# A graph-attention kernel on one core: gathers into the tile of three superchunks before, chunk by chunk behind the sums, instead of into a new tile

## Chip, core and metric

The kernel runs on one core of a Trainium2 chip. The metric is the device time of one execution in microseconds (us). Engines are named as in the profile: PE (TensorE, matmul), DVE (VectorE), ACT (ScalarE), POOL (GpSimd), SP (SyncE, DMA issue).

## The reference

Two graph-attention (GAT) layers over one graph of 6250 nodes with 256 features and 200 000 edges, which come sorted by destination `dst`, with 32 features on each edge. Layer 0 has 4 heads, layer 1 one.

```python
h = relu(layernorm(x))
for each layer:
    te = relu(edge_attr @ We + be) * exp(x @ Wo + bo)[src]      # 64 wide
    # self loops are added, each with the mean of its node's te
    hx, he = x @ Wg, te @ Wge
    al = leaky_relu((hx·a_s)[src] + (hx·a_d)[dst] + he·a_e, 0.2)
    al = exp(al - segment_max(al, dst)[dst]);  al /= segment_sum(al, dst)[dst]
    x  = segment_sum(hx[src] * al, dst) + b + x                 # relu behind layer 0
return input + h_after_both
```

So each edge needs the transformed row `hx[src]` of its source, weighted by a softmax over the edges of its destination, and summed per destination.

## The kernel before

The node rows of a layer stand in a table `T` in device memory (`T0`, `T1` for the layers): 256 features and a few columns that the logits need, 268 numbers a row in layer 0 and 260 in layer 1. The edges are cut into 1563 chunks of 128, and these into superchunks of C = 24, 66 in a layer (the last two of a layer have 17 and 10 chunks). A superchunk is a step; the 132 steps of both layers are numbered k = 0 to 131, and layer 1 begins with step 66.

What a step does:

- `gather` (L1066, POOL): one indirect DMA for each chunk, which brings 128 rows of `T`, picked by the edges' `src`, into `G[:, c, :]`. `G` is 128 x 24 x 270 float32. Three pools with one buffer each (`gath0` to `gath2`, `self.gp`) hold these tiles; step k uses pool k % 3, so steps k and k+3 share their memory. POOL's stream of instructions is little else than gathers.
- `logits`, `ends`, `links`, `maxima` (DVE, with short transposes on PE, L1305, L1371, L1388, L1564 among them): logits and the running maximum of each destination, by scans over sorted edges (L1381 is one of the scans).
- `scale` (layer 0, DVE, L1455) or `scale_rows` (layer 1, ACT, L1464): the gathered rows are multiplied by their weights.
- `onehots` (DVE, L1284): a one-hot matrix `S` of 128 x 128 for each chunk, from edge to node of the superchunk's window.
- `sums` (PE, L1474): 24 matmuls, one for each chunk, `u += S[c].T @ G[c]`, 48 records in the trace. They are the last readers of `G`.
- `evict` (ACT, L1479): `u` from PSUM to `U` in SBUF. The profile's chains end in this wait most often.
- `finish` of the step before, and `edge_rows` (PE, ACT: L1166, L1167, L1175) for the next: work that fills in between.

The loop over the steps is `edges`. In iteration k it calls `gather` for step k+1. POOL has its own queue and no other work, so a gather starts as soon as its waits allow; the program's order on the other engines doesn't hold it. Every DMA of POOL also waits for one of eight completion semaphores (DMASW0 to 7, used in turn).

A step's tile of `G` is made in one of two ways. Ordinarily it is a new tile of its pool. The first gather into it then waits for the whole tile of the step three before to be free: for PE's last sum of that step, and for DVE. This first gather is that of the last chunk; the rest follow in order 0 to 22. For steps 3, 4 and 5, and for some at the seam of the layers (steps 66, 68 and 69, in `ending` and `sources`), `st["own"]` names the older tile itself, and `gather` goes through the chunks in order 0 to 23. Each gather is then an ordinary overwrite of one chunk, and waits for that chunk's last reader alone.

A sum that something waits for increments PE's semaphore. In layer 0 most superchunks of before have one increment of 24 behind the last sum; behind the sums of layer 1, and of layer 0's steps 0 to 2, it is one of 1 behind each.

Of the kernel before, what the change touches and what calls it, by code (L numbers as in the profile page):

```python
# [81 lines left out]
class Kernel:  # L82
# [705 lines left out]
    def edges(self, ctx):  # L788
        nc = self.nc
        steps = self.steps  # L790
        if self.NS % 2:
            self.load_lb(1)
        pv = late = None
        self.ahead, self.rest = 1, None
        for k, st in enumerate(steps):
            nx = steps[k + 1] if k + 1 < len(steps) else None
            if st["s"] + 2 >= self.NS:
                continue
            for q in steps[k + 1:k + 3]:
                if q["L"] is st["L"] and "tw" not in q:  # L800
                    self.nodes(q)
            self.load_lb(k + 2)
            left = 99
            if self.ahead < len(self.groups):
                left = self.groups[self.ahead][0] - 2 - (self.ahead + 2 >= len(self.groups)) - k
            if self.rest is None and left <= 2:
                gi = self.index_load(self.ahead, self.xp)
                self.rest = self.index_group(self.ahead, self.xp, gi)
            if st["L"].l and (st["s"] == 2 or st["s"] + 3 == self.NS) and not hasattr(self, "flag_i"):
                self.flag()  # L810
                if self.early:
                    self.window()
            if st["s"] + 3 == self.NS:
                self.ending(st, *steps[k + 1:k + 3], pv, late, steps[k + 3] if k + 3 < len(steps) else None)
                pv = late = None
                continue
            if 3 <= k + 1 < 6 and nx["L"].l == 0:
                nx["own"] = steps[k - 2]["G"]
            if k:
                self.gather(nx)  # L820
                st["rows"] = st["L"].l
                drain(self.logits(st))
                self.ends(st)
            self.spread(nx)
            self.parts(nx)
            y = self.rphase1(nx)
            next(y)
            if k:
                self.links(st)
            if late:  # L830
                self.rows2(late)
            self.load_fl(k + 1)
            self.blocks(nx)
            if k:
                drain(self.maxima(st))
            drain(y)
            self.load_ea(k + 2)
            self.rphase2(nx)
            self.adst(nx)
            if "S" not in st:  # L840
                self.onehots(st)
            if k:
                if st["rows"]:
                    self.scale_rows(st)
                else:
                    drain(self.scale(st))
                self.carried(st)
                self.sums(st)
            if late:
                self.rows3(late)  # L850
                late = None
            self.onehots(nx)
            if pv:
                drain(self.finish(pv))
            self.evict(st)
            if pv:
                self.rows1(pv)
                late = pv
            self.index_on(left)
            if k == 4 and self.early:  # L860
                self.lacking()
            if k >= 6:
                next(self.late, None)
                next(self.late, None)
            self.edge_rows(nx)
            if st["s"] + 4 == self.NS:
                drain(self.finish(st))
            pv = st
# [186 lines left out]

    def gather(self, st):
        nc, L = self.nc, st["L"]
        own, G = "own" in st, st.get("own")
        if not own:
            G = self.G0 if st["k"] == 0 else self.gp[st["k"] % 3].tile([P, C, 270], F32, name="G")  # L1060
        st["G"] = G
        idx = self.src[:, st["o"]:st["o"] + st["C"]]
        last = st["C"] - 1
        c0 = (self.CX, self.CX1, 0)[min(st["k"], 2)]
        for c in range(last + 1) if own else (last, *range(c0, last)) if c0 <= last else ():
            nc.gpsimd.indirect_dma_start(  # L1066
                out=G[:, c, 0:L.TW], out_offset=None, in_=st.get("from", self.T[L.l])[0:self.N, :],
                in_offset=bass.IndirectOffsetOnAxis(ap=idx[:, c:c + 1], axis=0))
# [688 lines left out]
def drain(g):  # L1757
    for _ in g:
        pass
# [85 lines left out]
```

## Time and profile before

| | |
|---|---|
| time, median of 3 runs | 4930.62 us (4925.73 to 4934.31) |
| profiled execution | 4919.58 us |
| its span, first to last instruction | 4917.8 us |
| mean granted TensorE clock | 0.729 |
| busy: PE / PE weight load / DVE / ACT / POOL | 2927.7 / 1837.1 / 2461.0 / 1132.4 / 2988.8 us |
| gathers on POOL (L1066) | 3066 + 24, mean 950 ns |

The profile is of one execution; its page has been read together with answers of the trace: waits (the group that waited and its releaser, then us in total, times, longest us), groups of instructions by line, and timelines of an engine within a window. In a timeline a row begins with the start and the duration in us, and the bracket holds the idle time of the engine ahead of it and what ended it. "issue" is time in which the engine waited for nothing that the profile shows; "remote" is a releaser that it could not name.

### The profile page before, as it was taken

The page shows a single profiled execution, that of the slowest core. Times are in us where ns is not written, and L with a number is a line of the kernel's source. Part 1 is how long each engine was busy: PE and PEld are TensorE (multiplying, and loading weights), DVE is VectorE, ACT ScalarE, POOL GpSimd, SP SyncE. Part 2 cuts the span into 40 slices and gives each one's busy share as a digit, 9 for nine tenths or more (in the row PEclk, how much of TensorE's full clock was granted, in tenths as well). Part 3 has the DMA queues.
Part 4 walks back from the last instruction along what each step waited for, and adds up shares of the span by engine and source line. Part 5 has one row for each costly group of instructions (what it writes and reads, how often), then busy time and mean ns, then how long its engine had stood idle before and what let it go on. Part 6 is the DMA issues. An engine that isn't in the chain of part 4 may idle for free.

```text
span 4917.8 us, 38116 instructions
## 1 busy us (share of the span) xinstructions
PE 2927.7 (60%) x10100; PEld 1837.1 (37%) x10100; DVE 2461.0 (50%) x6148; ACT 1132.4 (23%) x2703; POOL 2988.8 (61%) x3216
## 2 busy tenths in 40 slices
PE   6656666666665666565646556555565555555556
PEld 5433433334343434343434333333333333333334
DVE  5556666666766666666744333333333332333335
ACT  4211111111111111111103333233332333323332
POOL 5356666666666666666554656666666665666663
PEclk8777777777777777777777666667676666766667
DMA  7144444444444444444433434444444443444442
GB/s 223 55 121 121 128 130 135 124 132 134 131 126 128 136 125 132 128 135 123 122 110 93 122 106 116 120 114 111 112 119 114 113 123 105 116 120 111 115 115 71
DMA packets 248252, 591.96 MB, mean 120 GB/s; under 512 B 65849, under 2 KB 105125, under 8 KB 247783
## 3 DMA queue, kind: packets, MB, share of 16 engines
q0 software_dynamic: 150048, 422.51, 32.8%
q1 hardware_dynamic: 97009, 164.82, 10.6%
q10 hardware_dynamic: 976, 2.12, 0.2%
q8 instruction: 86, 1.41, 0.1%
q14 instruction: 133, 1.09, 0.1%
HBM read 544.23 MB, written 45.36 MB: 120 GB/s over the span
## 4 chain that ended last, share of the span: by engine, by line
PE 30%; issue 28%; DVE 22%; POOL 10%; another core or an unknown queue 6%; DMA 2%; ACT 2%; DVEq 0%; ACTq 0%; POOLq 0%
PE u L1474 22%; POOL G L1066 10%; DVE G L1455 8%; PE y L1166 3%; DMA G<-T,src 2%; DVE S L1284 2%; PE zad L1175 2%; DVE m L1403 1%; PE ps L567 1%; DVE lb L1190 1%; ACT R L1167 1%; DVE rt L1333 1%; DVE fb L1398 0%; PE zad L1319 0%
## 5 line engine op out<-in xcount | busy, mean ns | idle before, releaser
L1066 POOL DMA_INDIRECT G<-T,src x3066 | 2913.0, 950 | 1817.8 <-issue 950.7
L1474 PE MATMUL u<-G,S 128*128 128x270 f32 (+1 forms) x6232 | 1866.5, 446 | 1421.0 <-issue 1194.1
L1474 PEld LDWEIGHTS u<-G,S 128*128 128x128 f32 x6232 | 1355.1, 220 | 1857.8 <-issue 1392.1
L1464 ACT ACTIVATE G<-G,kw 128x256 f32<-128x256 f32 x1512 | 609.0, 496 | 0.0
L1381 DVE TENSOR_TENSOR_SCAN cl<-fl,cl,lf 4x129 f32<-4x129 f32 (+1 forms) x130 | 61.1, 470 | 999.3 <-PE zad L1305 928.9
L1479 ACT ACTIVATE U<-u 128x270 f32<-128x270 f32 (+1 forms) x131 | 51.4, 393 | 2164.8 <-PE u L1474 1622.8
L1455 DVE TENSOR_TENSOR G<-G,kps 128x6144 f32<-128x6144 f32 (+6 forms) x86 | 441.7, 5149 | 0.0
L1284 DVE TENSOR_TENSOR S<-kps,loc 128x3072 f32<-128x3072 f32 (+1 forms) x135 | 438.1, 3245 | 4.7
L1166 PE MATMUL y<-ea,webd 64*128 64x256 f32 (+2 forms) x1056 | 355.2, 763 | 41.8 <-ACT R L1167 33.9
L1175 PE MATMUL zad<-R,wea 128*64 128x384 f32 (+1 forms) x1056 | 279.5, 666 | 156.6 <-ACT R L1167 84.9
L1167 ACT ACTIVATE R<-y,webd 128x1024 f32<-128x1024 f32 (+3 forms) x264 | 235.4, 892 | 428.3 <-PE y L1166 159.8
L1175 PEld LDWEIGHTS zad<-R,wea 128*64 128x64 f32 x1056 | 81.8, 174 | 392.5 <-issue 234.5
L1506 DVE SCALAR_TENSOR_TENSOR mg<-U,mw 128x1 f32<-128x1 f32 x66 | 14.6, 221 | 369.2 <-remote 160.7
L1166 PEld LDWEIGHTS y<-ea,webd 64*128 64x128 f32 x1056 | 115.9, 269 | 106.2 <-issue 60.3
L1333 DVE STREAM_TRANSPOSE rt<-zad 128x768 f32<-128x768 f32 (+1 forms) x130 | 125.8, 967 | 5.0 <-remote 5.0
L567 PE MATMUL fin<-wg,h1T 128*128 128x260 f32 x264 | 116.5, 586 | 1.6 <-ACT h1T L1566 1.6
L1190 DVE TENSOR_TENSOR lb<-lb,kps 128x1536 bf16<-128x1536 bf16 (+1 forms) x68 | 112.9, 1661 | 0.0
L1437 DVE SCALAR_TENSOR_TENSOR G<-U,kw,G 1x257 f32<-1x257 f32 x62 | 29.5, 476 | 152.5 <-issue 78.5
L1576 ACT ACTIVATE t1rows<-t1rows 128x1 f32<-128x1 f32 x66 | 13.4, 203 | 365.2 <-DVE crow L1443 144.3
L1564 PE MATMUL fin<-ident,fb 128*128 128x128 f32 x132 | 42.7, 379 | 79.9 <-issue 78.3
L1371 PE MATMUL lf<-ident,fb 128*36 128x128 f32 (+1 forms) x132 | 52.0, 394 | 59.9 <-DVE fb L1364 56.9
L1516 ACT ACTIVATE mw<-mw 128x8 f32<-128x8 f32 x66 | 13.8, 209 | 299.9 <-issue 137.9
(264 smaller groups left out, 2402.9 us busy)
## 6 DMA issues: line engine op xcount, KB each, us to landing
ea<-in_ea_dram SPq DMA_DIRECT2D x64, 768.0 KB
G<-T,src POOLq DMA_INDIRECT x3066
lb<-locrow SPq DMA_DIRECT2D x64, 384.0 KB
nd<-t1rows SPq DMA_DIRECT2D x66, 225.8 KB
tw<-nd SPq DMA_DIRECT2D x66, 225.8 KB
tw<-T SPq DMA_DIRECT2D x66, 117.2 KB
T<-t1rows SPq DMA_DIRECT2D x66, 113.8 KB
tw<-in_x_dram SPq DMA_DIRECT2D x66, 112.0 KB
```

What stands on the lines that cost most here:

```text
L567: self.nc.tensor.matmul(ps[:, :L.MW], hT[:, k, :], self.wg[L.l][:, k, :], start=(k == 0), stop=(k == 1))
L1066: nc.gpsimd.indirect_dma_start(out=G[:, c, 0:L.TW], out_offset=None, in_=st.get("from", self.T[L.l])[0:self.N, :], in_offset=bass.Indirect ...
L1166: nc.tensor.matmul(y[:, i, :n], self.webd[l][r, :], ea[r, w], start=True, stop=True)
L1167: nc.scalar.activation(R[:, :, w], y[:, :, :n], AF.Relu, bias=self.be[l])
L1175: nc.tensor.matmul(st["zad"][i * PH:(i + 1) * PH, o], self.wea[l][0], R[:, i, w], start=True, stop=False)
L1190: V.tensor_tensor(lb[:, :, :n], lb[:, :, :n], self.k_part.unsqueeze(2).to_broadcast([P, i, n]), op=OP.is_equal)
L1284: nc.vector.tensor_tensor(st["S"][:, c0:c1, :], self.k_iota.unsqueeze(1).to_broadcast(w), self.loc[:, o + c0:o + c1].unsqueeze(2).to_broad ...
L1333: V.transpose(rv[:, :32 * c].rearrange("p (b n) -> p b n", b=2), z.rearrange("p (b n) -> p b n", b=2)[:, :, :16 * c])
L1381: V.tensor_tensor_scan(cl[:H, :], fl[:H, :], lf[:H, 0:P + 1], init, op0=OP.add, op1=OP.max)
L1455: nc.vector.tensor_tensor(v, v, pw[:, c0:c1, :].unsqueeze(3) .to_broadcast([P, c1 - c0, H, L.F]), op=OP.mult)
L1464: self.nc.scalar.activation(v, v, AF.Copy, scale=st["w"][:, c:c + 1])
L1474: nc.tensor.matmul(st["u"][:, :L.W], S[:, i, :], G[:, i, 0:L.W], start=(j == 0), stop=(j == c - 1))
```

## The change

`gather` itself now sets `own` for every step above 2 that doesn't have it yet, to the tile of the step three before, and the place in `edges` that set it for steps 3 to 5 goes. So from the fourth superchunk on, in both layers, no new tile of `G` is taken, the chunks come in order 0 to 23, and each gather waits for PE's sum of the same chunk, three superchunks before.

```diff
@@ -814,8 +814,6 @@
                 self.ending(st, *steps[k + 1:k + 3], pv, late, steps[k + 3] if k + 3 < len(steps) else None)
                 pv = late = None
                 continue
-            if 3 <= k + 1 < 6 and nx["L"].l == 0:
-                nx["own"] = steps[k - 2]["G"]
             if k:
                 self.gather(nx)
                 st["rows"] = st["L"].l
@@ -1055,6 +1053,8 @@
 
     def gather(self, st):
         nc, L = self.nc, st["L"]
+        if st["k"] > 2 and "own" not in st:
+            st["own"] = self.steps[st["k"] - 3]["G"]
         own, G = "own" in st, st.get("own")
```

The order of instructions on PE, DVE, ACT and SP is the same in both programs. On POOL the same gathers are issued, with the last chunk of each superchunk at its end and no longer at its start, and with other waits. POOL, before, from one superchunk of layer 0 into the next (`G_2899`, `G_3076` are the two tiles, `T0_60` the table of layer 0, the list behind "waits" the semaphores):

```order
L1066 DMA G_2899<-T0_60,src_177 128x268 [waits DMASW7_49]
L1066 DMA G_3076<-T0_60,src_177 128x268 [waits DMASW0_49,DVE_49,PE_49]
L1066 DMA G_3076<-T0_60,src_177 128x268 [waits DMASW1_49]
L1066 DMA G_3076<-T0_60,src_177 128x268 [waits DMASW2_49]
L1066 DMA G_3076<-T0_60,src_177 128x268 [waits DMASW3_49]
L1066 DMA G_3076<-T0_60,src_177 128x268 [waits DMASW4_49]
```

The second row is the gather of the last chunk, and the only one that waits for PE. At the same place in the program after the change (`G_1912` and `G_206` are tiles of earlier superchunks, used again):

```order
L1066 DMA G_1912<-T0_60,src_177 128x268 [waits DMASW7_49,PE_49]
L1066 DMA G_206<-T0_60,src_177 128x268 [waits DMASW0_49,PE_49]
L1066 DMA G_206<-T0_60,src_177 128x268 [waits DMASW1_49,PE_49]
L1066 DMA G_206<-T0_60,src_177 128x268 [waits DMASW2_49,PE_49]
L1066 DMA G_206<-T0_60,src_177 128x268 [waits DMASW3_49,PE_49]
L1066 DMA G_206<-T0_60,src_177 128x268 [waits DMASW4_49,PE_49]
```

Every gather now has a wait on PE, each for another count, and the wait on DVE is gone. On PE, each sum of every superchunk that a later gather overwrites has an increment of 1; in all, 3086 sums increment the semaphore where 1757 did before, and the counts add up to the same.

## The prediction

> **What bounds the kernel now.** I read the busy time and the chain of the page first, then the waits, then the timelines of POOL, PE and ACT over one superchunk of each kind.
>
> ```profile
> span 4917.8 us, 38116 instructions
> PE 2927.7 (60%) x10100; PEld 1837.1 (37%) x10100; DVE 2461.0 (50%) x6148; ACT 1132.4 (23%) x2703; POOL 2988.8 (61%) x3216
> PE 30%; issue 28%; DVE 22%; POOL 10%; another core or an unknown queue 6%; DMA 2%; ACT 2%; DVEq 0%; ACTq 0%; POOLq 0%
> L1066 POOL DMA_INDIRECT G<-T,src x3066 | 2913.0, 950 | 1817.8 <-issue 950.7
> ACT U L1479 <- PE u L1474: 1622.8, 94, 22.2
> POOL G L1066 <- PE zad L1305: 382.4, 59, 8.2
> POOL G L1066 <- PE fin L1564: 212.6, 36, 25.0
> POOL G L1066 <- PE u L1474: 200.8, 44, 23.6
> ```
>
> No engine is busy for more than 61% of the span, so a loop of waits sets the pace. Two of them meet here. ACT's eviction of the sums (L1479) waits for PE. POOL's gather (L1066) pauses 139 times for the end of PE's sums (59, 36 and 44; the name is that of the last PE work that the trace saw), 795.8 us in all: this is the wait that the change goes for. A pause and the burst behind it, with the sums beside them, in layer 1; the columns are start, duration, engine, line, operation, tiles, and in brackets the idle time before it:
>
> ```profile
> 3491.99 0.39 ACT L1479 ACTIVATE U<-u 128x261 f32<-128x261 f32 x1 [21.51 <-PE u L1474]
> 3492.22 0.94 POOL L1066 DMA_INDIRECT G<-T,src  x1 [6.92 <-PE zad L1305]
> 3493.47 0.94 POOL L1066 DMA_INDIRECT G<-T,src  x1 [0.30 <-issue]
> 3497.75 8.52 PE L1474 MATMUL u<-G,S 128*128 128x261 f32 x38
> 3511.62 0.59 PE L1474 MATMUL u<-G,S 128*128 128x261 f32 x1 [2.68 <-issue]
> 3523.58 0.60 PE L1474 MATMUL u<-G,S 128*128 128x261 f32 x1 [0.84 <-issue]
> 3524.97 2.00 PE L1474 MATMUL u<-G,S 128*128 128x261 f32 x3 [0.79 <-issue]
> 3521.08 0.94 POOL L1066 DMA_INDIRECT G<-T,src  x1 [0.30 <-issue]
> 3527.04 0.39 ACT L1479 ACTIVATE U<-u 128x261 f32<-128x261 f32 x1 [21.36 <-PE u L1474]
> 3527.27 0.94 POOL L1066 DMA_INDIRECT G<-T,src  x1 [5.25 <-PE zad L1305]
> 3535.85 8.34 PE L1474 MATMUL u<-G,S 128*128 128x261 f32 x36
> ```
>
> A gather follows the last at 3493.47 − 3492.22 = 1.25 us, so a superchunk's 24 take 30.0. PE does the first 38 of its 48 records (two for a chunk) in 8.52 us, and then, with POOL's burst running, issues one every 1.4 to 3 us though it waits for nothing shown. POOL's last gather ends at 3522.02; the sums are through 5 us later, and the eviction comes at 3527.04. Only then may POOL start again. So the loop is: burst of 30.0 us, some 5 us in which PE catches up, next burst. The eviction is late because the burst holds PE back, not because PE has much to do.
>
> How long that loop takes on average, from the first and last eviction of a stretch in each layer and the number of them:
>
> ```profile
> 309.02 0.40 ACT L1479 ACTIVATE U<-u 128x270 f32<-128x270 f32 x1 [22.55 <-remote]
> 2433.94 0.40 ACT L1479 ACTIVATE U<-u 128x270 f32<-128x270 f32 x1 [3.25 <-PE u L1474]
> L1479 ACT ACTIVATE U<-u x60: 396/396/398, 336.1 to 2433.9; 128x270 f32<-128x270 f32 x60
> 2635.79 0.39 ACT L1479 ACTIVATE U<-u 128x261 f32<-128x261 f32 x1 [26.34 <-remote]
> 4859.35 0.39 ACT L1479 ACTIVATE U<-u 128x261 f32<-128x261 f32 x1 [13.49 <-PE u L1474]
> L1479 ACT ACTIVATE U<-u x62: 389/389/391, 2656.6 to 4859.4; 128x261 f32<-128x261 f32 x62
> ```
>
> Layer 0: (2433.94 − 309.02)/60 = 35.4 us a superchunk. Layer 1: (4859.35 − 2635.79)/62 = 35.9.
>
> **The change, part by part.** What it removes: the new tile at each superchunk, and the whole-tile wait with it. What it adds: a wait on PE in each gather of a step above 2, cleared by the sum of that chunk; on PE, an increment behind each chunk's sum where one behind the last had done. What it moves: the last chunk's gather from first to last place, which costs nothing, since the next reader of these rows comes two superchunks on; and POOL's burst, which may now start with the sums of the superchunk three back instead of with their end. PE, DVE, ACT and SP keep their order. Behind a waiting gather on POOL stand only gathers.
>
> Before already does this at a few places (its steps 3 to 5, and 69 in layer 1), and there the cost can be read. Sums of steps 1 and 2, which release gathers 4 and 5:
>
> ```profile
> 241.32 12.89 PE L1474 MATMUL u<-G,S 128*128 128x270 f32 x48 [2.17 <-DVE G L1445]
> 242.81 0.94 POOL L1066 DMA_INDIRECT G<-T,src  x1 [21.40 <-issue]
> 262.86 0.94 POOL L1066 DMA_INDIRECT G<-T,src  x1 [0.30 <-issue]
> 267.13 0.95 POOL L1066 DMA_INDIRECT G<-T,src  x1 [3.33 <-remote]
> 267.04 0.40 ACT L1479 ACTIVATE U<-u 128x270 f32<-128x270 f32 x1 [17.84 <-remote]
> 278.25 11.21 PE L1474 MATMUL u<-G,S 128*128 128x270 f32 x48 [1.25 <-DVE G L1445]
> 279.25 0.94 POOL L1066 DMA_INDIRECT G<-T,src  x1 [3.67 <-PE u L1474]
> 301.89 0.95 POOL L1066 DMA_INDIRECT G<-T,src  x1 [0.30 <-issue]
> 304.27 0.94 POOL L1066 DMA_INDIRECT G<-T,src  x1 [1.44 <-remote]
> ```
>
> And the sums of step 66, which release gather 69, with those of step 67 and step 3, where POOL lies idle:
>
> ```profile
> 2603.31 11.33 PE L1474 MATMUL u<-G,S 128*128 128x261 f32 x48
> 2630.86 0.94 POOL L1066 DMA_INDIRECT G<-T,src  x1 [0.30 <-issue]
> 2633.23 0.94 POOL L1066 DMA_INDIRECT G<-T,src  x1 [1.42 <-remote]
> 2645.85 10.72 PE L1474 MATMUL u<-G,S 128*128 128x261 f32 x48
> 323.14 12.89 PE L1474 MATMUL u<-G,S 128*128 128x270 f32 x48 [1.94 <-DVE G L1445]
> 336.07 0.40 ACT L1479 ACTIVATE U<-u 128x270 f32<-128x270 f32 x1 [4.79 <-PE u L1474]
> ```
>
> With POOL idle (step 3) the sums run from 323.14 to 336.03, and the eviction follows at 336.07: 12.9 us. Where the burst starts with the sums, PE's records end just as early (254.2, 289.5, 2614.6), but the eviction comes at 267.04, 309.02 and 2635.79. POOL's own waits tell why: it goes on at 1.25 us for 17, 19 and 22 gathers (until 262.86, 301.89 and 2630.86), then finds a chunk not released whose sum had ended over 8 us before; the eviction comes 3 to 6 us after that stop. So what is late is not the sum but the word of it, and a running burst holds that back. Start of the sums to eviction:
> - step 1: 267.04 − 241.32 = 25.7 us
> - step 2: 309.02 − 278.25 = 30.8 us
> - step 66: 2635.79 − 2603.31 = 32.5 us
>
> Mean 29.7. I take the mean, since none of the three differs in what runs beside it in a way that the rows show, and keep 25.7 and 32.5 as ends.
>
> The rest of the loop is from the eviction to the next sums (links, maxima, scaling). Layer 0: 278.25 − 267.04 = 11.2 us, while POOL's rest of a burst ran. Layer 1: 3535.85 − 3527.04 = 8.8 in the steady loop, 2645.85 − 2635.79 = 10.1 behind the burst of gather 69; I take 9.4 between them. These steps can't start earlier than the eviction, and POOL, having done its 24, then idles until the next sums: the pause doesn't go, it moves to behind the burst.
>
> Sum:
> - layer 0: 11.2 + 29.7 = 40.9 against 35.4 a superchunk; 5.5 × 60 = +329
> - layer 1: 9.4 + 29.7 = 39.1 against 35.9; 3.2 × 62 = +200
> - the last two superchunks of each layer have 17 and 10 chunks, hence short bursts: I take two of each layer out, 2 × (5.5 + 3.2) = −17
>
> Together +512 on the profiled run of 4919.58 (its span and 1.8 us around it): 5432. That run lies 0.2% under the median of the runs, about the 0.2% (10 us) below which a measurement of this kernel can't tell a difference; I give 5430.
>
> Ends. All like step 1: layer 0 36.9 (+89), layer 1 35.1 (−47): 4962. All like step 66, with 10.1 in layer 1: 43.7 and 42.6, (8.3 × 60 + 6.7 × 62) = +913: 5833. The loop breaks even where the sums' eviction comes 24.2 us (layer 0) and 26.5 us (layer 1) after their start, which is about where POOL is stopped at its 17th chunk as in step 1; each chunk that it gets further costs 1.25 us a superchunk.
>
> The wait itself costs POOL nothing: waiting and not waiting, gathers follow at 1.25 us (242.81 and after, 3492.22 and after).
>
> **A rule against the row.** The Trainium skill (SBUF — State Buffer, section "Who interferes with whom") says that a DMA never contends with a compute engine. By it, sums beside a burst would be evicted as in step 3, and the kernel would go to the first rival's time. The three rows above disagree: 25.7 to 32.5 us where POOL alone was added.
>
> **Rivals.**
> 1. *The word gets through; faster.* If the increments of all 24 chunks pass before the burst holds them back, which must happen within some 13 us of the sums' start, the eviction comes 12.9 us after it (step 3), the loop is 11.2 + 12.9 = 24.1 us, less than a burst, and POOL becomes the bound at 24 × 1.25 = 30.0. Then 4919.6 − 5.4 × 60 − 5.9 × 62 = 4230; part of the way, anything down to there. For it: PE's records do end in time. Against: in three of three samples the eviction was late. It decides below 24 us.
> 2. *Only the increments cost; the same or slightly slower.* If the samples' lateness is their neighbourhood's and not the burst's, what remains is one increment more per chunk. The rows bound it: the sums of step 3, with one increment behind the last, and those of step 1, with one behind each, both take 12.89 us; so between nothing and, taking the 2.2 us by which 12.89 stands above step 67's 10.72 as the most that such rows differ for other reasons, 2.2 × 60 = +132 in layer 0 (in layer 1 nearly every sum of before has its increment): 4920 to 5052. The Trainium skill (TensorE: Matmul & The Clock Gate, section "The cost: per-tile semaphore tail") says that increments on each matmul serialise at 26.3 ns and that one on the last is enough; by it 24 would be an estimated 0.6 us a superchunk, and the total some 4957. No row here shows that price alone.
> 3. *Nothing moves; the same.* The data of a gather is ready long before its reader, and only 10% of the chain is POOL. If the loop were closed by DVE and PE alone, the burst's place would not matter: 4920 to 4931. Against it: the eviction follows POOL's last gather by 5 us in the steady loop, and came after 12.9 us with POOL idle.
>
> **How the numbers follow.** Forecast case, sums held back as in the samples: 0.87. Rival 1: 0.06. Rival 2: 0.04. Rival 3: 0.03. The range is the forecast case's ends, 4960 to 5830, which also holds the dearer half of rival 2; rivals 1 and 3, the rest of rival 2 and what lies beyond the ends are left out, some 0.16. Faster 0.07 (rival 1, and a steady state stopped earlier than step 1), same 0.03 (rival 3), slower 0.90.
>
> **What would show it.** In the profile after, the idle time of L1066 should go from 139 pauses behind the eviction to two kinds: a few microseconds at a chunk between the 16th and the 23rd of each superchunk, just ahead of the eviction, and a longer one, up to some 9 us, between the burst's end and the next sums. The eviction should stand 26 to 33 us behind the start of its sums, PE's records of which should end in 11 to 13. POOL's busy time stays at 2913. I am wrong if POOL is stopped well before its 16th chunk, or if the eviction follows PE's last record directly; and in size, if the three samples aren't typical of a loop in which every burst is so placed.

## The result, and the profile after

The changed kernel takes 5823.41 us (median of 4 runs, 5795.48 to 5835.89) against 4928.17 us before (4916.81 to 4934.31): a ratio of 1.1825, interval 1.1802 to 1.1849. It is slower, as forecast, inside the range and close to its upper end; 5430 had been expected. The profiled run took 5828.29 us.

From the page of the changed kernel: the span, the busy times, the chain by engine, and the group of the gathers (busy us and mean ns | idle us before them, its largest releaser):

```profile
span 5826.5 us, 40936 instructions
PE 2733.8 (47%) x10100; PEld 1756.1 (30%) x10100; DVE 2463.0 (42%) x6148; ACT 1134.6 (19%) x2703; POOL 2991.7 (51%) x3216
another core or an unknown queue 38%; DVE 23%; issue 16%; ACT 11%; PE 11%; DMA 1%; POOL 0%; DVEq 0%; SPq 0%; ACTq 0%; POOLq 0%
L1066 POOL DMA_INDIRECT G<-T,src x3066 | 2916.1, 951 | 2692.6 <-PE u L1474 1524.8
```

The work is unchanged: POOL's gathers are busy for 2916 us (2913 before), DVE and ACT as before, PE somewhat less. The granted TensorE clock is lower, 0.684 against 0.729, but PE is busy for 194 us less all the same, so PE's own work is not what grew. What grew is the gathers' idle time, from 1817.8 to 2692.6 us, which is 875 of the 909 us by which the span grew. From the waits of the changed kernel (who waited for whom, us, times, longest):

```profile
ACT U L1479 <- remote: 2623.9, 116, 27.8
DVE cl L1381 <- remote: 2070.2, 115, 26.3
POOL G L1066 <- PE u L1474: 1562.9, 454, 38.2
POOL G L1066 <- remote: 370.2, 476, 4.7
```

The eviction and the scan behind it wait about 20 us in nearly every superchunk for a releaser that the trace can't name: PE's instruction had long ended by its record. A superchunk of layer 1, from its timeline (sums, the burst that they release, the eviction, the scan, a step of DVE behind the scan, the next sums):

```profile
4614.56 12.07 PE L1474 MATMUL u<-G,S 128*128 128x261 f32 x48
4615.91 0.95 POOL L1066 DMA_INDIRECT G<-T,src  x1 [11.22 <-PE u L1474]
4632.19 0.94 POOL L1066 DMA_INDIRECT G<-T,src  x1 [0.30 <-issue]
4634.88 0.95 POOL L1066 DMA_INDIRECT G<-T,src  x1 [1.75 <-remote]
4646.24 0.95 POOL L1066 DMA_INDIRECT G<-T,src  x1 [1.63 <-remote]
4646.72 0.39 ACT L1479 ACTIVATE U<-u 128x261 f32<-128x261 f32 x1 [25.82 <-remote]
4647.44 0.47 DVE L1381 TENSOR_TENSOR_SCAN cl<-fl,cl,lf 1x129 f32<-1x129 f32 x1 [22.20 <-remote]
4647.49 0.95 POOL L1066 DMA_INDIRECT G<-T,src  x1 [0.31 <-remote]
4650.31 0.20 DVE L1398 TENSOR_TENSOR fb<-flpen,lf 128x48 f32<-128x48 bf16 x1 [1.75 <-remote]
4657.74 7.46 PE L1474 MATMUL u<-G,S 128*128 128x261 f32 x32
```

The sums' records end at 4626.63. POOL finds a chunk not released at 4633.1 and again at 4644.6, and the eviction comes at 4646.72, 32.2 us behind the sums' start. The scan follows 0.7 us later, but the step behind it (L1398), which reads a short transpose of PE (L1388), starts at 4650.31, 1.9 us behind the end of POOL's last gather (4648.44) and 2.9 behind the scan. Before, in the superchunk of layer 1 shown in the prediction, it starts 1.3 us behind its scan, which began at 3527.22:

```profile
3528.52 0.20 DVE L1398 TENSOR_TENSOR fb<-flpen,lf 128x48 f32<-128x48 bf16 x1 [0.20 <-PE lf L1388]
```

And one of layer 0, from the eviction to the next sums, with the same three instructions of before behind it (its eviction, its scan, its next sums):

```profile
1575.74 0.40 ACT L1479 ACTIVATE U<-u 128x270 f32<-128x270 f32 x1 [22.54 <-remote]
1577.09 0.95 POOL L1066 DMA_INDIRECT G<-T,src  x1 [0.30 <-issue]
1579.97 0.47 DVE L1381 TENSOR_TENSOR_SCAN cl<-fl,cl,lf 4x129 f32<-4x129 f32 x1 [20.29 <-remote]
1591.09 2.09 PE L1474 MATMUL u<-G,S 128*128 128x270 f32 x8 [1.15 <-DVE G L1445]
1592.08 0.95 POOL L1066 DMA_INDIRECT G<-T,src  x1 [14.04 <-PE u L1474]
```

```profile
1053.71 0.40 ACT L1479 ACTIVATE U<-u 128x270 f32<-128x270 f32 x1 [13.74 <-PE u L1474]
1054.35 0.47 DVE L1381 TENSOR_TENSOR_SCAN cl<-fl,cl,lf 4x129 f32<-4x129 f32 x1 [3.42 <-PE zad L1305]
1065.49 1.72 PE L1474 MATMUL u<-G,S 128*128 128x270 f32 x3 [3.27 <-issue]
```

From the scan to the next sums it is 11.1 us in both of these. But after the change the scan stands 4.2 us behind the eviction, and before 0.6. PE's words for the scan (the transposes behind the sums) stand behind the sums' own words. Here the eviction gets through while POOL issues its last gathers, and the scan starts only 1.9 us behind the end of the last (1578.04).

The loop, from the first and last eviction of the same stretches as before:

```profile
312.03 0.40 ACT L1479 ACTIVATE U<-u 128x270 f32<-128x270 f32 x1 [23.33 <-remote]
L1479 ACT ACTIVATE U<-u x60: 397/397/398, 358.4 to 2981.5; 128x270 f32<-128x270 f32 x60
L1479 ACT ACTIVATE U<-u x63: 390/390/391, 3182.8 to 5767.5; 128x261 f32<-128x261 f32 x63
```

Layer 0: (2981.5 − 312.0)/60 = 44.5 us a superchunk (35.4 before), layer 1: (5767.5 − 3182.8)/62 = 41.7 (35.9). That is +545 and +361, 906 us together: the whole of it is in these loops.

### The profile page after: what moved, and what is told of

Same layout as the page of the kernel before. It is cut to its first block, busy times and chain, and to the rows that moved or that the text cites. A ratio compares the mean times of both kernels' runs of the same rounds, so it can differ in the third digit from the quotient of the medians.

```text
span 5826.5 us, 40936 instructions
## 1 busy us (share of the span) xinstructions
PE 2733.8 (47%) x10100; PEld 1756.1 (30%) x10100; DVE 2463.0 (42%) x6148; ACT 1134.6 (19%) x2703; POOL 2991.7 (51%) x3216
## 4 chain that ended last, share of the span: by engine, by line
another core or an unknown queue 38%; DVE 23%; issue 16%; ACT 11%; PE 11%; DMA 1%; POOL 0%; DVEq 0%; SPq 0%; ACTq 0%; POOLq 0%
ACT G L1464 9%; DVE G L1455 7%; PE u L1474 4%; PE y L1166 3%; DVE S L1284 3%; DVE lb L1190 1%; ACT R L1167 1%; DVE rt L1333 1%; DVE m L1403 1%; PE ps L567 1%; PE lf L1388 1%; PE fin L567 1%; DVE al L1351 1%; PE zad L1175 0%
## 5 line engine op out<-in xcount | busy, mean ns | idle before, releaser
L1066 POOL DMA_INDIRECT G<-T,src x3066 | 2916.1, 951 | 2692.6 <-PE u L1474 1524.8
L1474 PE MATMUL u<-G,S 128*128 128x270 f32 (+1 forms) x6232 | 1556.6, 412 | 146.4 <-DVE G L1445 130.2
L1474 PEld LDWEIGHTS u<-G,S 128*128 128x128 f32 x6232 | 1267.9, 205 | 443.5 <-DVE G L1445 166.0
L1388 PE MATMUL lf<-ident,cl 36*128 36x36 f32 (+1 forms) x132 | 41.3, 313 | 2114.5 <-issue 1171.4
L1381 DVE TENSOR_TENSOR_SCAN cl<-fl,cl,lf 4x129 f32<-4x129 f32 (+1 forms) x130 | 61.3, 471 | 2190.4 <-remote 2070.2
L1388 PEld LDWEIGHTS lf<-ident,cl 36*128 36x128 f32 (+1 forms) x132 | 23.4, 178 | 2175.5 <-issue 1204.9
L1166 PE MATMUL y<-ea,webd 64*128 64x256 f32 (+2 forms) x1056 | 373.0, 796 | 227.5 <-ACT R L1167 199.2
L1175 PE MATMUL zad<-R,wea 128*64 128x384 f32 (+1 forms) x1056 | 349.3, 811 | 176.3 <-ACT R L1167 173.6
L1175 PEld LDWEIGHTS zad<-R,wea 128*64 128x64 f32 x1056 | 96.9, 207 | 478.6 <-ACT R L1167 368.6
L1398 DVE TENSOR_TENSOR fb<-flpen,lf 128x192 f32<-128x192 bf16 (+1 forms) x132 | 36.6, 278 | 241.4 <-remote 188.4
L567 PE MATMUL fin<-wg,h1T 128*128 128x260 f32 x264 | 134.7, 664 | 1.6 <-ACT h1T L1566 1.6
L1371 PE MATMUL lf<-ident,fb 128*36 128x128 f32 (+1 forms) x132 | 39.2, 297 | 162.3 <-DVE fb L1364 100.8
```

Source lines behind the costliest of these rows:

```text
L567: self.nc.tensor.matmul(ps[:, :L.MW], hT[:, k, :], self.wg[L.l][:, k, :], start=(k == 0), stop=(k == 1))
L1066: nc.gpsimd.indirect_dma_start(out=G[:, c, 0:L.TW], out_offset=None, in_=st.get("from", self.T[L.l])[0:self.N, :], in_offset=bass.Indirect ...
L1166: nc.tensor.matmul(y[:, i, :n], self.webd[l][r, :], ea[r, w], start=True, stop=True)
L1175: nc.tensor.matmul(st["zad"][i * PH:(i + 1) * PH, o], self.wea[l][0], R[:, i, w], start=True, stop=False)
L1388: nc.tensor.transpose(pc, cl[:n, 0:P], self.ident[0:n, 0:n])
L1474: nc.tensor.matmul(st["u"][:, :L.W], S[:, i, :], G[:, i, 0:L.W], start=(j == 0), stop=(j == c - 1))
```

## The experiments

The theory: a running burst of gathers holds back what PE has to say to the other engines, whatever the waits; started with the sums, the burst stands in front of the scan and scaling, not beside them. (PE's "word" is its semaphore's increment as another engine sees it.) Against it stood the price of the waits and increments, the reuse of the tile itself, and the data in flight. Kernels are compared with before on the chip on which they ran (4855.73, 4947.06 and 4862.65 us in the three groups of runs).

**Last chunk first again.**

```diff
-        for c in range(last + 1) if own else ...
+        for c in (last, *range(last)) if own else ...
```

> The changed kernel with the last chunk's gather of each superchunk first again (order 23, 0 to 22), so that the first gather waits for the last sum and the others find theirs done; tiles are still those of three steps before. Theory (the burst's start is what costs: started with the sums it runs in front of the scan, scaling and one-hots instead of beside them): the burst starts behind the eviction again, the loop is back at 35.4 and 36.0 us, the time at 4930, 4900 to 4960. Rival (using the old tile itself, or one gather's wait on PE, costs): stays near 5820. Rival (the increments cost): part of the way, 5000 to 5700, if the sums keep them.

4826.61 us, ratio 0.9935 (0.9913 to 0.9957), and 0.9929 (0.9906 to 0.9953) when run once more:

> The run with the last chunk first again, on the chip of these runs, so that the row of first chunks 11 to 23 can be compared: 0.990 to 0.997.

The 4900 to 4960 us expected for the first run were 0.994 to 1.006 of before; it came just under. So taking the old tile costs nothing; the order of one gather is worth the whole 18%. It does two things at once, though. The burst starts behind the last sum, and as the wait for that sum covers all others of the superchunk, POOL's semaphore instructions at the gathers, of which the trace counts 245 before and 3009 after the change, are down to 279. This run alone doesn't tell the start from the waits. The waits of this kernel are again of before's kind:

```profile
POOL G L1066 <- PE zad L1305: 347.7, 58, 20.3
POOL G L1066 <- PE u L1474: 176.1, 26, 26.9
POOL G L1066 <- PE fin L1564: 157.0, 33, 8.7
```

680.8 us against 795.8. Why it is 0.7% faster than before wasn't followed up.

**One wait a superchunk.** The rows are short, 64 numbers, and all go into chunk 0's place in four parts:

```diff
+        less = own and 5 < st["s"] < self.NS - 6
+        if less:
+            src = src.rearrange("n d -> (n d)")[0:self.N * 64].rearrange("(n d) -> n d", d=64)
...
+                out=G[:, 0, c % 4 * 64:][:, 0:64] if less else G[:, c, 0:L.TW], out_offset=None, in_=src,
```

> The changed kernel, but in 108 of the superchunks every gather brings 64 numbers a row and writes into chunk 0's place of the tile, so that only the first gather waits for PE (for sum 0) and PE has no other increments for gathers. The burst still starts with the sums, and nothing stops it midway; rows and what is computed are not the reference's. Theory (a running burst holds back what PE has to say, whatever the waits): eviction 30 to 36 us behind the start of the sums, period 43 to 47 us, 5650 to 6050. Rival (the 24 waits and increments are what is late): eviction 13 us behind the start, POOL bounds the loop at 30 us, about 5823 - 108 x 13.4 = 4380.

5357.32 us (one run), 1.103 times before on its chip: between the two. Both expectations were missed; with nothing to stop it POOL sometimes ran two bursts together and sometimes paused between them. Sums, POOL's last gather, and the eviction of a superchunk in which POOL didn't stop, one of the latest evictions of layer 0:

```profile
1331.97 11.65 PE L1478 MATMUL u<-G,S 128*128 128x270 f32 x40 [4.82 <-DVE crow L1447]
1344.00 0.39 PE L1478 MATMUL u<-G,S 128*128 128x270 f32 x1 [0.37 <-issue]
1346.79 0.59 PE L1478 MATMUL u<-G,S 128*128 128x270 f32 x1 [2.40 <-issue]
1349.60 0.61 PE L1478 MATMUL u<-G,S 128*128 128x270 f32 x1 [2.22 <-issue]
...
1368.49 0.37 PE L1568 MATMUL fin<-ident,fb 128*128 128x128 f32 x1 [2.42 <-issue]
1370.67 0.94 POOL L1070 DMA_INDIRECT G<-T,src  x1 [0.30 <-issue]
1378.55 0.40 ACT L1483 ACTIVATE U<-u 128x270 f32<-128x270 f32 x1 [36.23 <-remote]
```

No gather waits for these sums beyond the first, and still PE issues one record every 2.8 us under the burst, and the eviction comes 7 us behind POOL's stop at 1371.6, 46.6 us behind the sums' start. So a burst can hold PE's words back without the 24 waits and increments. It does so less often than in the changed kernel: of these 108 superchunks, 31 have their eviction more than 30 us behind the sums' start, where the changed kernel has 71 of the same ones. Nor does a burst always hold the words to its end: with sums from 608.09 to 619.93 the eviction came at 626.55, 17 us into a burst in which POOL went on without a pause, and in 13 of the 108 POOL had so gone on from the start of the sums to the eviction. With one wait the kernel loses 10%, not 18%; whether the waits and increments add to the lateness, or POOL's running ahead takes some of it away, stays open.

**Short rows, all waits.** As the last, but each gather in its own chunk's place (`out=G[:, c, 0:64 if less else L.TW]`).

> The changed kernel, but in the same 108 superchunks a gather brings 64 numbers a row instead of 268 or 260, into the place of its own chunk, with every wait as changed; rows and what is computed are not the reference's. Theory (POOL's issuing holds PE's word back, not the data moved): the same 128 rows take POOL as long, the time stays within 1.5% of 5823. Rival (the gathered data in flight is what PE and its word compete with): a quarter of the data, so most of the lateness goes: eviction some 15 to 20 us behind the sums' start, 4400 to 5000.

5842.4 us (one run), the changed kernel's time; that is 1.203 times before on its chip, where the change was 1.1825, but the loops are 44.8 and 41.7 us, as there. POOL's group (min, median and max ns) and the queue of its gathers (packets, MB, share) with short rows:

```profile
L1070 POOL DMA_INDIRECT G<-T,src x3066: 942/947/1207, 95.8 to 5779.1; - x192
q0 software_dynamic: 108576, 157.09, 13.7%
```

The same queue in the changed kernel:

```profile
q0 software_dynamic: 150048, 422.51, 28.1%
```

With 37% of the bytes, a gather takes POOL as long (947 ns median) and the loop too. So it isn't the amount of data that PE's word competes with. That leaves POOL's issuing or the transfers as such: the queue still has 72% of its packets, and no run here issues gathers without moving rows.

**The first chunk as a scale.** If only the burst's start counts, it can be set anywhere: the gather of chunk m goes first, then 0 to m − 1, then the rest.

```diff
+        m = min(11, last)
+        for c in (m, *range(m), *range(m + 1, last + 1)) if own else ...
```

> The changed kernel with the order 11, 0 to 10, 12 to 23: the burst starts behind sum 11 of the superchunk three before, 5 to 6 us later than behind sum 0. Theory (burst and the stage behind the eviction stand one after the other): the loop gets longer by the later start, less some of the stops midway (2 to 4 us a superchunk): 122 x 2 to 122 x 5.5 more, 6050 to 6500. Rival (fewer waits that matter, less meeting of burst and sums): faster than the changed kernel, 5200 to 5800.

4791.35 us against 4855.73: faster than before (one run, 0.987), where the theory had said slower than the changed kernel, and faster than the rival's 5200 to 5800 too. A later start isn't simply added: behind sum 11 the rest of the sums and the scan still get their words through while the burst is young (in this run's layer 0 the eviction comes 0.05 us behind the end of the sums' records on average), and the loop of before comes back. The next runs asked where the edge is:

> As the run from chunk 11, but first chunk 17 (order 17, 0 to 16, 18 to 23). Theory, as the run from chunk 11 left it (words of PE still pass in the first 6 us or so of a burst; the burst may start when the sums that remain then fit into that): 6 sums remain, 3 us, so evictions stay close behind the burst's start, periods between those of the runs from 23 and from 11, 34.6 to 35.6; ratio to before 0.985 to 0.995. Rival (an earlier start is always better while the first chunk isn't 0): also between. This run sets the slope.

> The run from chunk 11 again, timed: 12 sums remain, 6 us, which just fits. Ratio to before 0.980 to 0.992.

> First chunk 8: 15 sums remain, 7.5 us. Theory of the first 6 us: over the edge in part of the superchunks, whose eviction then comes only behind the burst: ratio 1.00 to 1.10. Rival (earlier is better): 0.975 to 0.985.

> First chunk 5: 18 sums remain, 9 us. Theory of the first 6 us: like the changed kernel, evictions behind the burst in nearly all superchunks, 1.08 to 1.19 times before. Rival (earlier is better): 0.97 to 0.98.

> First chunk 14, between the runs from 11 (0.995) and from 17 (0.977): 0.977 to 0.990 if nothing else happens between; it shows where the edge is.

> First chunk 20, between the runs from 17 (0.977) and from 23 (0.9935): 0.978 to 0.992.

| first chunk | us | ratio to before | interval | POOL's semaphore instructions at the gathers |
|---|---|---|---|---|
| 0 (the change) | 5823.41 | 1.1825 | 1.1802 to 1.1849 | 3009 |
| 5 | 5687.63 (one run) | 1.150 | | 2507 |
| 8 | 5022.50 | 1.0147 | 1.0126 to 1.0168 | 2129 |
| 11 | 4920.33 | 0.9952 | 0.9936 to 0.9969 | 1754 |
| 14 | 4751.07 | 0.9773 | 0.9749 to 0.9797 | 1378 |
| 17 | 4830.55 | 0.9769 | 0.9752 to 0.9785 | 1004 |
| 20 | 4749.38 | 0.9777 | 0.9753 to 0.9800 | 635 |
| 23 (last first) | 4824.50 | 0.9929 | 0.9906 to 0.9953 | 279 |

The edge lies between 5 and 11, and from 14 to 20 it is flat. (The kernel from chunk 11 gave 0.987 on one chip and 0.9952 on another, so ratios from different chips compare to about 0.01.) The expectations for 5, 8 and 14 held; 11 came 0.003 above its interval, 17 came 0.008 below and 20 by a hair below.

The waits fall along this scale as the start moves back. The run with one wait a superchunk parts the two: it has 843 semaphore instructions, fewer than the run from chunk 17 with its 1004, and is 10% slower than before where that one is 2.3% faster. So the number of waits can't be all of the cause; where the burst starts matters. What goes wrong below the edge, from first chunk 5 in layer 0 (sums, start of the burst, eviction, ACT and PE of the next stage, next sums, next burst):

```profile
1045.17 12.26 PE L1475 MATMUL u<-G,S 128*128 128x270 f32 x48
1049.49 0.95 POOL L1067 DMA_INDIRECT G<-T,src  x1 [13.15 <-PE u L1475]
1057.46 0.40 ACT L1480 ACTIVATE U<-u 128x270 f32<-128x270 f32 x1 [12.07 <-PE u L1475]
1064.60 2.08 PE L1167 MATMUL y<-ea,webd 64*128 64x512 f32 x4 [4.22 <-ACT R L1168]
1083.49 1.11 ACT L1168 ACTIVATE R<-y,webd 128x1024 f32<-128x1024 f32 x1 [16.24 <-remote]
1088.04 11.32 PE L1475 MATMUL u<-G,S 128*128 128x270 f32 x48
1091.42 0.94 POOL L1067 DMA_INDIRECT G<-T,src  x1 [11.99 <-PE u L1475]
```

The sums get through 8 us into the burst, so my edge of 6 us for them was too small. It is the next stage that doesn't: `y` is done by its record at 1066.7, 17 us into the burst, and its reader `R` starts at 1083.49, 16.8 us later and 4 behind POOL's stop (1091.42 − 11.99 = 1079.43). So it is not one threshold: here the words early in the burst pass and a late one waits for its end. What counts, as far as these rows go, is that all of a superchunk's chain, sums and next stage, falls into the part that passes. With first chunk 17, in layer 1:

```profile
3298.24 0.94 POOL L1067 DMA_INDIRECT G<-T,src  x1 [5.19 <-PE u L1475]
3301.30 0.39 ACT L1480 ACTIVATE U<-u 128x261 f32<-128x261 f32 x1 [20.94 <-PE u L1475]
3306.98 7.97 PE L1475 MATMUL u<-G,S 128*128 128x261 f32 x35
3333.22 0.95 POOL L1067 DMA_INDIRECT G<-T,src  x1 [5.00 <-PE u L1475]
```

The burst starts 3.1 us ahead of the eviction instead of 0.2 behind it, the next sums 5.7 us behind the eviction, and the loop is 3333.22 − 3298.24 = 35.0: the 30.0 of the burst and a pause of 5.0.

**One stop in the middle.** The change as it is, but with the last chunk's gather in the thirteenth place:

```diff
+        h = (last + 1) // 2
+        for c in (*range(h), last, *range(h, last)) if own else ...
```

> The changed kernel with one gather moved: the order is 0 to 11, then 23, then 12 to 22. The burst still starts with the sums, and 23 of 24 gathers keep their place and wait, but POOL must stop in the middle for the last sum's word. Theory (POOL's going on without a stop is what holds back PE's words): the stop, some 16 us behind the sums' start, lets them out; eviction 18 to 22 us behind the start, the next stage beside the second half of the burst, periods of 34 to 36 us: ratio to before 0.97 to 1.03. Rival (starting the burst with the sums costs in itself): close to the changed kernel, 1.12 to 1.19.

4844.80 us, ratio 0.9979 (0.9943 to 1.0015): no different from before. Here is a superchunk in which the burst starts with the sums, as in the changed kernel (sums, burst's start, eviction, and POOL's next gather behind its stop):

```profile
1030.48 11.56 PE L1475 MATMUL u<-G,S 128*128 128x270 f32 x48
1031.83 0.95 POOL L1067 DMA_INDIRECT G<-T,src  x1 [8.95 <-PE u L1475]
1049.03 0.40 ACT L1480 ACTIVATE U<-u 128x270 f32<-128x270 f32 x1 [16.20 <-remote]
1049.27 0.94 POOL L1067 DMA_INDIRECT G<-T,src  x1 [2.60 <-remote]
```

POOL stops at 1046.67, 16 us behind the sums' start and 15 into the burst, and 2.4 us later the eviction is there, 18.5 behind the sums' start. One gather moved takes away the change's whole loss, and this superchunk shows how: a stop of 2.6 us lets the word out. Two things keep it from being a clean test. Only 31 of 117 superchunks of the two layers have such a start (113 in the changed kernel); in the others the loop has shifted, and in 83 POOL is already issuing gathers when the sums begin. In the 31, the eviction comes after 17.0 us in layer 0 and 18.6 in layer 1 on average (the changed kernel's: 29.3 and 30.1). And the wait for the last sum covers those for sums 12 to 22, so that POOL has 1643 semaphore instructions at the gathers and not 3009, about as many as the run from chunk 11 (1754, 0.9952). So the 31 speak against the rival that starting with the sums costs in itself; that the stop alone brought the whole gain is not shown.

## Why the prediction was right, and where its size was off

The direction, the mechanism and its main term held. The eviction behind the start of the sums, for which the mean of three samples gave 29.7 us, was 29.4 in layer 0 and 30.0 in layer 1 on average over the same stretches as the loops; POOL is stopped late in a burst and the sums' records end in 12 us, as the prediction's last part asked for; and the pauses went where it said, 14.04 us in layer 0 and 11.22 in layer 1 between the burst and the next sums, against "up to some 9".

The step that was mis-sized is the rest of the loop, from the eviction to the next sums, which the sum took as 11.2 us in layer 0 and 9.4 in layer 1. It measured 15.2 and 11.7 on average. That is 4.0 us and 2.3 us too little; times 60 and 62 it makes some 380 of the 396 us by which the change of the profiled run (+909) passed the forecast's +512. Means over the 60 and 62 superchunks, in us:

| stretch | layer 0 before | after | layer 1 before | after |
|---|---|---|---|---|
| eviction to scan (L1381) | 1.6 | 2.4 | 0.3 | 0.8 |
| scan to the step that reads PE's next short transpose (L1398) | 1.4 | 2.9 | 1.3 | 3.7 |
| that step to the next sums | 9.9 | 9.9 | 6.5 | 7.3 |

So the rest grew mostly in the two places where the chain waits for a short transpose of PE. In layer 0 the sample was also short: 11.2, where before's own mean is 12.9 (some waits for the scan are long; their median is 0.6, after the change 2.1). I took the eviction as the moment at which everything of PE gets out, on a single superchunk in layer 0 and two in layer 1; but PE's words behind the sums' can be late once more when POOL goes on with the rest of its burst, as in the two superchunks above. "These steps can't start earlier than the eviction" was true, and not enough. That 5823 still lies under the upper end of 5830 is luck: this end was high because it took the latest of three evictions for every superchunk, which they were not, and so made room for a term that was too small. One of the four runs took 5835.89.

The first rival (words get through in time, faster) was wrong for chunk 0 first, but not absurd: with first chunks 14 to 20 the words of the sums that are left get through early in the burst (the eviction 3.1 us behind its start in the superchunk shown) and the kernel is 2% faster. It isn't down to POOL's bound of 30.0 us a superchunk: in that superchunk POOL still pauses for 5.0 us. The second (the increments cost) put their price at +132 us at most, against the +909 measured, and the third (nothing moves) fell too. Whether the waits and increments add to the lateness of PE's words, which the second didn't ask, is what the run with one wait left open.

The page that spoke against the forecast, the Trainium skill's SBUF — State Buffer, section "Who interferes with whom", says that a DMA never contends with a compute engine. As to the amount of data the runs agree: with 37% of the bytes the time stayed. But under a burst the matmuls' records stand 2.8 us apart and PE's words come late. Whether that comes from the transfers or from the engine that issues them, of which the sentence doesn't speak, no run here tells.

## What to carry to other kernels

A wait that is made finer lets an engine start earlier, and so moves when it runs; ask which chain it ran beside before, and which it will now stand in front of. Where a long run of POOL gathers and a chain of short dependent steps share a loop, the gap between the bursts is no waste: in the kernel before it is when PE's late words come out (the eviction 5 us behind POOL's last gather in the superchunk of layer 1), and its place was worth more than its length (18%). Try the point of release as a scale and not as all or nothing: the best of it, chunks 14 to 20, was 2.2 to 2.3% faster than before.

## What the runs showed of the hardware that I had not expected

- While POOL issues indirect DMAs one after another (0.95 us each, every 1.25 us), PE can fall to one matmul record every 2.8 us, and its completions reach ACT, DVE and POOL late, some only when POOL stops: 2.4 us after the stop with PE done, 5 to 7 with work queued. An early end of PE's records is then no proof that its readers could start; the profile's page calls these ends modelled, so the runs don't tell whether the sum itself or its signal is late.
- It is not the bytes: with 37% of them the time is the same. Nor does it need many semaphore increments: with one for the gathers in a superchunk the same crawl is there. What in POOL's issuing, or in its transfers, holds PE back stays open.
- PE's crawl began behind 38 of the 48 records in the row of before, 14 us into a burst, and behind 40 in the run with one wait, 26 us behind POOL's last pause. So the age of the burst alone doesn't set it off; what does, no run here shows.
